# Block-wise scatters and paired turns in an expert stage, and gathers tied to the scores of the group in front

## The chip, the core and the metric

The kernel runs on one core of a Trainium2 chip. The core has five engines that work side by side, each with its own queue of instructions in a fixed order: PE (TensorE, matmuls and transposes), DVE (VectorE), ACT (ScalarE), POOL (GpSimd) and SP (SyncE, which here only issues DMAs). They wait for each other by semaphores. The metric is the time of one execution on the device, in microseconds (us); less is better.

## The reference, cut to what matters

The program is two layers of attention and feed-forward on 1024 tokens (32 sequences of 32) of 256 values, all in float32. The change lies in the last two stages. The first of these is attention over a paged cache of keys and values with a window of 128 positions, the second a mixture of 16 experts of which each token uses two, with one shared expert beside them:

```python
scores = jnp.where(allowed[:, None, None, :, :], scores, -jnp.inf)
p = jax.nn.softmax(scores, axis=-1)
o = jnp.einsum('bghts,bgsd->bghtd', p, v_all).reshape(Bx, H, Tx, HD)
...
topk_val, topk_idx = jax.lax.top_k(probs, TOPK)          # TOPK = 2, E = 16
w = topk_val / (jnp.sum(topk_val, axis=-1, keepdims=True) + EPS)
g = jnp.einsum('th,ehi->tei', xt, Wg)
u = jnp.einsum('th,ehi->tei', xt, Wu)
y = jnp.einsum('tei,eih->teh', jax.nn.silu(g) * u, Wd)
routed = jnp.einsum('tke,tk,teh->th', oh, w, y)
shared = jax.nn.silu(xt @ sWg) * (xt @ sWu) @ sWd
return (routed + shared).reshape(b, s, h)
```

## The kernel before, in words

The kernel is one unrolled program. A scheduling layer orders each engine's instructions; `behind(a, b)` (L185) tells it that b has to stand behind a on the same engine, without a semaphore, and `tc.add_manual_dep(..., waits, ...)` adds a true wait.

**The paged stage** takes 8 groups of 4 sequences. `begin(g)` issues five gathers of 128 rows of 1 KB on POOL (L1098), one for each sequence's window and one (a = 4, issued first in the code) for the new rows of all four, into a buffer `kv` of which there are four. It turns keys and queries on PE. `score` (L1157) makes the scores of one sequence, masks them on DVE, takes the exponential on ACT and lets POOL copy a part aside (`pl`, L1176). `values` turns the weights, copies them on ACT (`PT`, L1188) and multiplies by the values (L1191); `end` finishes a group (L1198 to L1225). From group 2 on, the a = 4 gather of a group waits for the first product with the values of the group two in front (`valued[g - 2]`, L1105). The gathers of groups 0 and 1 have no such wait. POOL executes its queue in order, so a gather that waits holds up every gather and `pl` copy behind it.

**The experts.** A router picks two experts for each token, which makes 2048 rows. They are sorted by expert and cut into 16 blocks of 128 rows (`NB`). A block can hold rows of several experts, so a *piece* is a block together with one expert that has rows in it; there are at most 31 (`NP` = 16 + 16 - 1), and the program always runs 31. Which block and expert a piece has is known only at run time; PE and DVE load the numbers into registers and address the weights `ew` and the rows `xT` with them. POOL picks the rows of the 16 blocks out of DRAM (`xg`, L1469, 16 indirect DMAs, nine ahead of the loop, the others in it).

The loop (from L1558, `for j in range(NP)`) does for each piece: while j < 16, two transposes of block j (`xt`, L1565) and a DVE copy to `xT` (L1567); a DVE copy of the piece's block by its register address (`xs`, L1576); two products with the gate and up weights (`gu`, L1579); silu on ACT (L1591) and the multiply on DVE (`hb`, L1592); a turn of the 128x128 result on PE (`ht`, L1594) and its copy on ACT (`hT`, L1596); the product with the down weights (`y`, L1598); a copy of that from PSUM to SBUF (`yb`, on DVE for odd j at L1601, on ACT for even j at L1603; twelve buffers). From j = 2 on POOL scatters the copy to the rows of `ys_d` in DRAM (L1608, 31 indirect DMAs). A row that is in the block but not of the piece's expert gets an index out of bounds (`SKIP`) and isn't written. `places()` works out these indices: one column for each piece.

The PSUM pool of `y` has two banks, those of `xt`, `gu` and `ht` two each; `xs` has three buffers. The order on PE in the first half is, for a pair of pieces: turn of the even piece, four transposes, product of the even piece, turn of the odd piece, product of the odd piece, eight gate and up products of the next pair.

Beside the loop runs the shared expert: `shared_in` (products `gu<-AVT,wfo`, silu, multiply) and `shared_out` (L1347, L1351) for each half of the tokens. The second half comes behind the loop. At the end 8 DMAs on the queues of SP and ACT load `ys_d` (L1628); they wait for the last scatter. DVE adds the rows by their weights (L1632), and 8 DMAs write the output (L1635).

Of the kernel before, what the change touches and what calls it, by code (L numbers as in the profile page):

```python
# [24 lines left out]
P = 128  # L25
# [103 lines left out]
def tile_layers(ctx: ExitStack, tc: tile.TileContext, i: dict, out: bass.AP):  # L129
# [916 lines left out]
    with tc.tile_pool(name="w1", bufs=1, reuse_waits="tile") as wp:  # L1046
# [31 lines left out]
        with (  # L1078
# [7 lines left out]

            valued = {}

            def begin(g):

# [4 lines left out]
                for a in (4, 0, 1, 2, 3):  # L1097
                    got = g_.indirect_dma_start(  # L1098
                        out=kv[:, a, :],
                        out_offset=None,  # L1100
                        in_=rows_d,
                        in_offset=bass.IndirectOffsetOnAxis(ap=at[:, g, a : a + 1], axis=0),
                    )
                    if a == 4 and g > 1:
                        tc.add_manual_dep(got.ins, valued[g - 2].ins.name, waits, reason="no long row of gathers")  # L1105
                q.KT = KT = sp.tile([P, 4, NPOS], F32, tag="KT", name="KT")

                def queries():
# [44 lines left out]
            def score(q, b):  # L1153

                ps = sc.tile([P, 2, NPOS], F32, tag="sc", name="sc")
                for h in range(2):
                    mm_ = te.matmul(  # L1157
                        ps[:, h, :],
                        lhsT=q.qz[:, b, h].rearrange("p g t -> p (g t)"),
                        rhs=q.KT[:, b, :],  # L1160
                        start=True,
                        stop=True,
                    )
                q.scored.append(mm_)
                sm = sp.tile([P, 2, NPOS], F32, tag="sm", name="sm", bufs=5)
                v.scalar_tensor_tensor(  # L1166
                    sm, bad[:, 4 * q.g + b, :].unsqueeze(1).broadcast_to([P, 2, NPOS]), NEG, ps, ALU.mult, ALU.add
                )
# [147 lines left out]
        with (  # L1316
# [3 lines left out]
            def small(name, shape, dt=F32):  # L1320
                return hp.tile(list(shape), dt, name=name)

            hs = small("h", (P, CH)), small("up", (P, CH))

            def shared_in(n, pool, tag, eng):
                ns = slice(n * CH, (n + 1) * CH)
                pair = []
                for f in (NE, NE + P):
                    ps = pool.tile([P, CH], F32, tag=tag, name=tag)
                    products([(ps, [(wfo[:, k, f : f + P], AVT[:, k, ns]) for k in range(2)])])  # L1330
                    pair.append(ps)
                h, up = hs if n == 0 else hs[::-1]
                silu = s.activation(h, pair[0], AF.Silu)
                for x in exps_:
                    behind(x, silu)
                if eng is g_:
                    s.copy(up, pair[1])
# [14 lines left out]

            w12 = small("w12", (P, 2, NG))
            eb = small("eb", (1, NP), I32)
            to = small("to", (P, NP), I32)
            xT = hp.tile([P, NB, D], F32, name="xT")
            with (
                tc.tile_pool(name="mm5", bufs=3, space=bass.MemoryType.PSUM, reuse_waits="tile") as mm,
# [6 lines left out]
                def rows_out(g):  # L1365

                    po = mm.tile([P, CH], F32, tag="mm", name="mm")
                    products([(po[:, :D], [(AVT[:, k, g * P : (g + 1) * P], wo2[:, k, :]) for k in range(2)])])
                    o = sp.tile([P, D], F32, tag="o", name="o")
# [143 lines left out]
            with (  # L1513
# [3 lines left out]
                tc.tile_pool(name="y5", bufs=2, space=bass.MemoryType.PSUM, reuse_waits="tile") as yp,  # L1517
            ):
                def places():

                    of = small("of", (P, NB, NE))
                    of_ = v.tensor_tensor(
                        of,
# [8 lines left out]
                    v.scalar_tensor_tensor(slot_, slot_, float(NT), tok_, ALU.mult, ALU.add)  # L1532
                    v.tensor_scalar(slot_, slot_, -SKIP, None, ALU.add)
                    mine = small("mine", (P, NP, NB))
                    v.tensor_tensor(
                        mine,
# [1 line left out]
                        C("piece").rearrange("p (j b) -> p j b", b=NB),  # L1538
                        ALU.is_equal,
                    )  # L1540
                    v.tensor_tensor(mine, mine, slot_.unsqueeze(1).broadcast_to([P, NP, NB]), ALU.mult)
                    tof = small("tof", (P, NP))
                    v.tensor_reduce(tof, mine, AX.X, ALU.add)
                    v.tensor_scalar(to, tof, SKIP, None, ALU.add)

                def weigh():

# [9 lines left out]
                put, ybs, gus = [], [], []  # L1557
                for j in range(NP):  # L1558
                    if j == 2:
                        places()  # L1560
# [33 lines left out]
                    te.transpose(ph[:, :P], h, ident)  # L1594
# [3 lines left out]
                    te.matmul(py[:, :D], lhsT=hT, rhs=w[:, 2 * D :], start=True, stop=True)  # L1598
                    yb = sp.tile([P, D], F32, tag="yb", name="yb", bufs=12)
                    if j % 2:  # L1600
                        v.tensor_copy(yb, py[:, :D])  # L1601
                    else:
                        s.copy(yb, py[:, :D])  # L1603
                    ybs.append(yb)
                    if j >= 2:
                        for k in range(len(put), j + 1):
                            put.append(
                                g_.indirect_dma_start(  # L1608
                                    out=ys_d,
                                    out_offset=bass.IndirectOffsetOnAxis(ap=to[:, k : k + 1], axis=0),  # L1610
                                    in_=ybs[k],
                                    in_offset=None,
                                    bounds_check=2 * NT - 1,
                                    oob_is_err=False,
                                )
                            )
                weigh()
                shared_out(1, shared_in(1, gp, "gu", v), yp, "y")
                behind(picked[-1], *put)
                for j, a in enumerate(put):  # L1620
                    for b in put[:j]:
                        tc.declare_no_dep(a.ins, b.ins, reason="a row is written by one piece")
# [86 lines left out]
```

## Time and profile before

| | us |
|---|---|
| runs of the kernel: median of 3 (lowest to highest) | 644.38 (643.24 to 644.47) |
| the profiled execution | 649.91 |
| its span | 647.7 |
| PE, DVE, POOL, ACT busy in the span | 579.4, 377.9, 195.7, 185.0 |
| paged stage, from its first gather to its last POOL copy | 437 to 535 |
| experts' pieces, from the first gate product to the last down product | 559 to 631 |
| loads of the scattered rows, sums and output | 634 to 647.7 |

All rows of the trace are times from the span's start in one profiled execution. A row of the timeline gives start, duration, engine, line, operation, `out<-in` by the program's names with sizes, how many, and in brackets the idle time in front of it and what ended it. PE's ends are modelled. In a float32 matmul a row often counts two passes ("x2"). A row of the windows gives what each engine was busy in a stretch, the clock that PE was granted (1.00 is full) and the share and speed of the DMA engines.

### The profile page before, as it was taken

The page shows a single profiled execution, that of the slowest core. Times are in us where ns is not written, and L with a number is a line of the kernel's source. Part 1 is how long each engine was busy: PE and PEld are TensorE (multiplying, and loading weights), DVE is VectorE, ACT ScalarE, POOL GpSimd, SP SyncE. Part 2 cuts the span into 40 slices and gives each one's busy share as a digit, 9 for nine tenths or more (in the row PEclk, how much of TensorE's full clock was granted, in tenths as well). Part 3 has the DMA queues.
Part 4 walks back from the last instruction along what each step waited for, and adds up shares of the span by engine and source line. Part 5 has one row for each costly group of instructions (what it writes and reads, how often), then busy time and mean ns, then how long its engine had stood idle before and what let it go on. Part 6 is the DMA issues. An engine that isn't in the chain of part 4 may idle for free.

```text
span 647.7 us, 9218 instructions
## 1 busy us (share of the span) xinstructions
PE 579.4 (89%) x3302; PEld 449.0 (69%) x3302; DVE 377.9 (58%) x880; ACT 185.0 (29%) x503; POOL 195.7 (30%) x279
## 2 busy tenths in 40 slices
PE   3989999999999998999999999996788889686992
PEld 1667778688778886788878886785565666464660
DVE  4656675865956939433292139554566685642535
ACT  1312232332312213122031103233456454121440
POOL 5014001523530049950000000007465300655550
PEclk9979999999999999999999999997799989797997
DMA  6962300555441000000000046014221101221115
GB/s 176 361 214 27 64 2 26 153 128 134 116 131 39 0 14 1 1 2 17 0 1 1 1 161 293 1 54 119 57 66 58 49 2 66 74 61 46 33 50 194
DMA packets 29884, 48.47 MB, mean 75 GB/s; under 512 B 8249, under 2 KB 21966, under 8 KB 29008
## 3 DMA queue, kind: packets, MB, share of 16 engines
q1 hardware_dynamic: 19405, 30.23, 13.7%
q0 software_dynamic: 5904, 15.39, 9.2%
q10 hardware_dynamic: 4531, 2.28, 1.2%
q8 instruction: 26, 0.43, 0.3%
q14 instruction: 18, 0.15, 0.1%
HBM read 36.84 MB, written 13.01 MB: 77 GB/s over the span
## 4 chain that ended last, share of the span: by engine, by line
PE 70%; DVE 16%; issue 4%; ACT 3%; DMA 3%; POOL 2%; another core or an unknown queue 1%; ACTq 0%; SPq 0%; DVEq 0%; POOLq 0%
PE ff L196 30%; PE mm L196 11%; PE gu L1579 4%; PE y L1598 3%; PE sc L1157 3%; PE tr L477 3%; DVE vblk L427 2%; PE sc L444 2%; PE po L1191 2%; PE mm L939 2%; DVE kb L437 2%; ACT sm L1172 2%; DVE AVT L1225 1%; PE tr L470 1%; POOL xg L1469 1%
## 5 line engine op out<-in xcount | busy, mean ns | idle before, releaser
L1098 POOL DMA_INDIRECT kv<-rows_d,at x40 | 39.2, 979 | 173.8 <-DVE rsm L1012 152.3
L662 POOL COPY rr<-raw 88x256 f32<-88x256 f32 x64 | 29.4, 493 | 95.8 <-PE tr L525 48.8
L594 DVE SCALAR_TENSOR_TENSOR th<-th,ff 128x512 f32<-128x512 f32 x32 | 21.8, 683 | 38.1 <-ACT th L593 38.1
L437 DVE TENSOR_TENSOR kb<-KT,con 128x1024 f32<-128x1024 f32 x28 | 34.0, 1234 | 12.3 <-ACT KT L539 6.0
L1608 POOL DMA_INDIRECT ys_d<-yb,to x31 | 30.8, 995 | 22.3 <-ACT hT L1596 7.4
L1579 PE MATMUL gu<-ew,xs 128*128 x124 | 36.4, 415 | 0.7 <-DVE xs L1576 0.7
L593 ACT ACTIVATE th<-ff 128x512 f32<-128x512 f32 x32 | 19.1, 597 | 59.5 <-PE ff L196 56.1
L196 PE MATMUL ff<-x,w_g 128*128 128x256 f32 x128 | 35.6, 391 | 0.0
L196 PE MATMUL ff<-x,w_u 128*128 128x256 f32 x128 | 34.9, 386 | 0.0
L196 PE MATMUL ff<-y,f_w_gate 128*128 128x256 f32 x128 | 31.5, 381 | 0.0
L196 PE MATMUL ff<-y,f_w_up 128*128 128x256 f32 x128 | 31.1, 381 | 0.3 <-DVE th L594 0.3
L1172 ACT ACTIVATE sm<-sm,mx 128x160 f32<-128x160 f32 x64 | 26.8, 420 | 11.7 <-DVE mx L1170 8.6
L196 PE MATMUL ff<-h,d_Wd 128*128 128x256 f32 x128 | 29.8, 381 | 0.0
L1598 PE MATMUL y<-ew,hT 128*128 x62 | 21.9, 436 | 7.7 <-issue 4.2
L196 PE MATMUL ff<-h,f_w_down 128*128 128x256 f32 x128 | 28.3, 379 | 0.0
L1157 PE MATMUL sc<-KT,qz 128*128 128x160 f32 x128 | 25.9, 335 | 2.6 <-issue 2.4
L1579 PEld LDWEIGHTS gu<-ew,xs 128*128 128x128 f32 x124 | 24.3, 209 | 5.6 <-DVE xs L1576 1.1
L1191 PE MATMUL po<-PT,kv 128*128 128x256 f32 x64 | 19.8, 432 | 9.4 <-ACT PT L1188 7.5
L1166 DVE SCALAR_TENSOR_TENSOR sm<-bad,sc 128x320 f32<-128x320 bf16 x32 | 15.5, 485 | 21.5 <-PE sc L1157 8.0
L196 PEld LDWEIGHTS ff<-x,w_g 128*128 128x128 f32 x128 | 22.8, 189 | 7.4 <-issue 4.9
L595 DVE SCALAR_TENSOR_TENSOR h<-th,ff 128x512 f32<-128x512 f32 x32 | 21.8, 680 | 9.4 <-PE ff L196 9.1
L196 PEld LDWEIGHTS ff<-x,w_u 128*128 128x128 f32 x128 | 23.5, 190 | 5.4 <-issue 2.2
(421 smaller groups left out, 1314.5 us busy)
## 6 DMA issues: line engine op xcount, KB each, us to landing
ew<-in_L_ffn_W SPq DMA_DIRECT2D x1, 6144.0 KB
rows_d<-rr SPq DMA_DIRECT2D x32, 176.0 KB
x<-in_x SPq DMA_DIRECT2D x4, 256.0 KB
w_u<-in_L_cond_Wu SPq DMA_DIRECT2D x1, 1024.0 KB
w_g<-in_L_cond_Wg SPq DMA_DIRECT2D x1, 1024.0 KB
d_Wd<-in_L_cond_Wd SPq DMA_DIRECT2D x1, 1024.0 KB
f_w_gate<-in_L_ffn_w_gate SPq DMA_DIRECT2D x1, 1024.0 KB
f_w_up<-in_L_ffn_w_up SPq DMA_DIRECT2D x1, 1024.0 KB
```

The source lines that it names most:

```text
L196: mm_ = te.matmul(ps, lhsT=a, rhs=b, start=j == 0, stop=j == len(pairs) - 1)
L437: v.tensor_tensor(kb, KT[:, m, js].rearrange("p (b k) -> p b k", b=4).unsqueeze(2).broadcast_to([P, 4, 8, 32]), m8.unsqueeze(1).unsqueeze( ...
L594: v.scalar_tensor_tensor(flat(t), flat(t), 1.0, flat(pg), ALU.add, ALU.mult)
L595: v.scalar_tensor_tensor(flat(h[:, f : f + 2]), flat(t), 0.5, flat(pu), ALU.mult, ALU.mult)
L662: g_.tensor_copy(r[:, :, j].rearrange("p o g d -> p g o d"), raw[j].rearrange("p (g a o d) -> a p g o d", g=4, a=8, d=32)[a],)
L1098: got = g_.indirect_dma_start(out=kv[:, a, :], out_offset=None, in_=rows_d, in_offset=bass.IndirectOffsetOnAxis(ap=at[:, g, a : a + 1], ax ...
L1157: mm_ = te.matmul(ps[:, h, :], lhsT=q.qz[:, b, h].rearrange("p g t -> p (g t)"), rhs=q.KT[:, b, :], start=True, stop=True,)
L1172: exp_ = s.activation(sm[:, h], sm[:, h], AF.Exp, bias=mx[:, h : h + 1], accum_out=q.su[:, b, h : h + 1])
L1191: mm_ = te.matmul(q.po[:, b, : 2 * P], lhsT=q.kv[:, b, P:], rhs=PT[:, j, :], start=True, stop=False)
L1579: mm_ = te.matmul(pg[:, :D], lhsT=x[:, 0, k * P : (k + 1) * P], rhs=w[:, k * D : (k + 1) * D], start=k == 0, stop=k == 1,)
L1598: te.matmul(py[:, :D], lhsT=hT, rhs=w[:, 2 * D :], start=True, stop=True)
L1608: g_.indirect_dma_start(out=ys_d, out_offset=bass.IndirectOffsetOnAxis(ap=to[:, k : k + 1], axis=0), in_=ybs[k], in_offset=None, bounds_ch ...
```

## The change

There are three parts.

*Scatters by block.* The result of a piece is no longer copied to a buffer of its own. A buffer `yall` of 16 blocks is set to zero by four POOL memsets ahead of the picks. Each piece's result is multiplied by a column of 0 and 1 (`own`: is the row of this piece?) and added into its block of `yall` on DVE, at an address from a register. Block b is complete with piece b + 15 at the latest, and then one scatter writes all its 128 rows; 16 scatters replace 31. `places()` gets shorter: the indices are one column for each block, without `SKIP`, and it stands one piece earlier.

*Pairs of turns.* For odd pieces up to j = 15 the turn (`ht`) has to stand ahead of the product `y` of the piece in front: turn, turn, product, product. The second half's `shared_in` products have to stand behind the last piece's product.

*Gathers.* The a = 4 gather of group 1 waits for the first score of group 0, and that of group 2 for the first score of group 1 in place of the first product with the values of group 0. The others stay.

```diff
-                    if a == 4 and g > 1:
-                        tc.add_manual_dep(got.ins, valued[g - 2].ins.name, waits, reason="no long row of gathers")
+                    if a == 4 and g:
+                        x = scored[g - 1] if g < 3 else valued[g - 2]
+                        tc.add_manual_dep(got.ins, x.ins.name, waits, reason="no long row of gathers")
...
+                scored.setdefault(q.g, mm_)
...
-                    products([(ps, [(wfo[:, k, f : f + P], AVT[:, k, ns]) for k in range(2)])])
+                    for k in range(2):
+                        up_ = te.matmul(ps, lhsT=wfo[:, k, f : f + P], rhs=AVT[:, k, ns], start=k == 0, stop=k == 1)
+                        if after:
+                            behind(after, up_)
...
-            to = small("to", (P, NP), I32)
+            to, own = small("to", (P, NB), I32), small("own", (P, NP))
+            yall = hp.tile([P, NB, D], F32, name="yall")
+            for b in range(0, NB, 4):
+                g_.memset(yall[:, b : b + 4, :], 0.0)
...
-                    v.tensor_tensor(mine, mine, slot_.unsqueeze(1).broadcast_to([P, NP, NB]), ALU.mult)
-                    tof = small("tof", (P, NP))
-                    v.tensor_reduce(tof, mine, AX.X, ALU.add)
-                    v.tensor_scalar(to, tof, SKIP, None, ALU.add)
+                    v.tensor_reduce(own, mine, AX.X, ALU.max)
+                    v.scalar_tensor_tensor(to, slot_, float(NT), tok_, ALU.mult, ALU.add)
...
-                    te.transpose(ph[:, :P], h, ident)
+                    ht_ = te.transpose(ph[:, :P], h, ident)
+                    if j % 2 and j < NB:
+                        behind(ht_, yd)
...
-                    te.matmul(py[:, :D], lhsT=hT, rhs=w[:, 2 * D :], start=True, stop=True)
-                    yb = sp.tile([P, D], F32, tag="yb", name="yb", bufs=12)
-                    if j % 2:
-                        v.tensor_copy(yb, py[:, :D])
-                    else:
-                        s.copy(yb, py[:, :D])
...
+                    yd = te.matmul(py[:, :D], lhsT=hT, rhs=w[:, 2 * D :], start=True, stop=True)
+                    ys_.append((j, at_b, py))
+                    if j == 1:
+                        places()
+                    while j >= 1 and ys_:
+                        k, at_k, py = ys_.pop(0)
+                        to_k = yall[:, bass.ds(at_k, 1), :].rearrange("p a n -> p (a n)")
+                        kept_.append(
+                            v.scalar_tensor_tensor(to_k, py[:, :D], own[:, k : k + 1], to_k, ALU.mult, ALU.add)
+                        )
+                    if j >= NE - 1:
+                        b = j - NE + 1
+                        put.append(
+                            g_.indirect_dma_start(
+                                out=ys_d,
+                                out_offset=bass.IndirectOffsetOnAxis(ap=to[:, b : b + 1], axis=0),
+                                in_=yall[:, b, :],
+                                in_offset=None,
+                            )
                         )
                 weigh()
-                shared_out(1, shared_in(1, gp, "gu", v), yp, "y")
+                shared_out(1, shared_in(1, gp, "gu", v, yd), yp, "y")
```

Two lines declare that the adds of later blocks and the scatter of an earlier one touch different rows, so that none waits for the other; the buffer `o` of the rows that are picked later now shares the three buffers of `xs`.

More of the change, by code (lines that the diff above doesn't have):

```diff
@@ L1085, in tile_layers @@
                 pass
-            valued = {}
+            scored, valued = {}, {}
             def begin(g):
@@ L1323, in tile_layers, with shared_in @@
             hs = small("h", (P, CH)), small("up", (P, CH))
-            def shared_in(n, pool, tag, eng):
+            def shared_in(n, pool, tag, eng, after=None):
                 ns = slice(n * CH, (n + 1) * CH)
@@ L1368, in rows_out @@
                     products([(po[:, :D], [(AVT[:, k, g * P : (g + 1) * P], wo2[:, k, :]) for k in range(2)])])
-                    o = sp.tile([P, D], F32, tag="o", name="o")
+                    o = sp.tile([P, 1, D], F32, tag="xs", name="o")[:, 0, :]
                     s.copy(o, po[:, :D])
@@ L1531, in places @@
                     v.tensor_tensor(pn, pn, C("block1"), ALU.add)
-                    v.scalar_tensor_tensor(slot_, slot_, float(NT), tok_, ALU.mult, ALU.add)
-                    v.tensor_scalar(slot_, slot_, -SKIP, None, ALU.add)
                     mine = small("mine", (P, NP, NB))
@@ L1555, in weigh @@
                     v.tensor_tensor(w12, w12, su.unsqueeze(1).broadcast_to([P, 2, NG]), ALU.mult)
-                put, ybs, gus = [], [], []
+                put, kept_, ys_, gus = [], [], [], []
                 for j in range(NP):
                     if j == 2:
-                        places()
                         shared_out(0, first_h, yp, "y")
@@ L1597, in tile_layers @@
                     py = yp.tile([P, CH], F32, tag="y", name="y")
-                    te.matmul(py[:, :D], lhsT=hT, rhs=w[:, 2 * D :], start=True, stop=True)
-                    yb = sp.tile([P, D], F32, tag="yb", name="yb", bufs=12)
-                    if j % 2:
-                        v.tensor_copy(yb, py[:, :D])
-                    else:
[L1603 to L1615, printed above, removed]
+                    yd = te.matmul(py[:, :D], lhsT=hT, rhs=w[:, 2 * D :], start=True, stop=True)
[16 more added lines that the diff above has]
+                                in_offset=None,
                             )
+                        )
                 weigh()
-                shared_out(1, shared_in(1, gp, "gu", v), yp, "y")
+                shared_out(1, shared_in(1, gp, "gu", v, yd), yp, "y")
                 behind(picked[-1], *put)
@@ L1621, in tile_layers @@
                     for b in put[:j]:
-                        tc.declare_no_dep(a.ins, b.ins, reason="a row is written by one piece")
+                        tc.declare_no_dep(a.ins, b.ins, reason="a row is in one block")
+                    for x in kept_[j + NE :]:
+                        tc.declare_no_dep(x.ins, a.ins, reason="a later block's rows")
                 ys = ys_d.rearrange("(k g p) d -> g p k d", k=2, p=P)
```

## The prediction

> **What bounds the kernel now.** I read the page first: PE is busy for 89% of the span and holds 70% of the chain that ended last. That is an average. The table of stretches shows the stages that the change touches (columns: PE, weight loads, DVE, ACT and POOL busy, granted clock, DMA share, GB/s):
>
> ```profile
> 437.00:470.00 33.00, 23.50 (x112) 17.54 (x111) 16.02 (x38) 13.68 (x46) 20.33 (x26) 0.79 0.31 88
> 568.60:603.00 34.40, 26.06 (x113) 18.43 (x111) 14.13 (x46) 8.10 (x30) 18.40 (x19) 0.90 0.17 54
> 603.00:628.40 25.40, 25.40 (x109) 17.33 (x109) 11.27 (x36) 11.51 (x40) 14.92 (x16) 1.00 0.13 42
> ```
>
> The rows are the start of the paged stage, the first half of the experts' pieces, and their second half. In the second half PE is never idle, at full clock. In the other two it is idle for 8 to 9 us and runs below full clock. So time can be won there, and no engine is the bound there. The timeline of the first half shows how. A pair of pieces that runs undisturbed:
>
> ```profile
> 579.01 0.32 PE L1594 MATMUL ht<-ident,hb 128*128 128x128 f32 x1
> 579.16 0.60 PE L1565 MATMUL xt<-ident,xg 128*128 128x128 f32 x4
> 579.74 0.70 PE L1598 MATMUL y<-ew,hT 128*128 x2
> 580.27 0.27 PE L1594 MATMUL ht<-ident,hb 128*128 128x128 f32 x1
> 581.06 0.70 PE L1598 MATMUL y<-ew,hT 128*128 x2 [0.52 <-ACT yb L1603]
> 581.60 1.89 PE L1579 MATMUL gu<-ew,xs 128*128 x8
> ```
>
> The next pair's first turn stands at 583.33, so a pair takes 4.32 us, 0.52 of it PE waiting for the second turned tile. Then one pair goes wrong:
>
> ```profile
> 583.77 0.99 POOL L1608 DMA_INDIRECT ys_d<-yb,to  x1 [0.30 <-issue]
> 584.06 0.70 PE L1598 MATMUL y<-ew,hT 128*128 x2
> 587.22 0.42 DVE L1567 COPY xT<-xt 128x256 f32<-128x256 f32 x1 [0.99 <-remote]
> 587.26 0.37 ACT L1603 COPY yb<-y 128x256 f32<-128x256 f32 x1 [3.26 <-remote]
> 588.34 1.22 PE L1598 MATMUL y<-ew,hT 128*128 x2 [3.48 <-issue]
> 589.36 3.62 PE L1579 MATMUL gu<-ew,xs 128*128 x8
> ```
>
> ACT's copy wants a product that PE began at 584.06 and gets it at 587.26, though ACT and DVE had nothing else to do. I call this a late handoff. PE then starves, the granted clock falls to 0.50 (587.0 to 593.5 in the windows), and eight gate products take 3.62 instead of 1.89. The next first turn stands at 594.39: the pair took 11.06 us, **6.74 more than a clean one**. What stands beside it is POOL: from 579.83 to 591.3 it issues ten scatters back to back, because the first nine had waited behind the picks (the last at 578.58). The start of the paged stage looks the same, with 14 gathers in a row:
>
> ```profile
> 453.73 0.95 POOL L1098 DMA_INDIRECT kv<-rows_d,at  x1 [0.31 <-issue]
> 457.20 0.49 DVE L1166 SCALAR_TENSOR_TENSOR sm<-bad,sc 128x320 f32<-128x320 bf16 x1 [7.58 <-remote]
> 457.26 0.59 ACT L1188 COPY PT<-tr 128x512 f32<-128x512 f32 x1 [6.01 <-remote]
> ```
>
> PE's transposes for that ACT copy ended at 453.4, so 3.8 us are lost there, and the clock after it. In 603 to 628 scatters come one per 1.65 us, each with a pause in front, and nothing is late.
>
> **Part 1, scatters by block.** 31 scatters (0.995 us each on POOL) become 16. The first stands behind piece 15, so none is issued between the last pick and about 599. The row of ten is gone. What that is worth is not in the trace; its bounds are 0, if the late handoff has another cause, and 6.74, if the row is all of it. One number pulls the value down: the profiled execution took 649.91 (span 647.7 and 2.2 around it), the runs' median is 644.38, so 5.53 us exist in the profiled execution only. The visible late time is some 17 us (8 around the gathers' row, where the first group took 21.7 us from first score to its end against 13.6 for the second; 6.7 here; about 1.2 at 570.6 to 571.8 and 1.0 at 564). If the 5.53 lies there in proportion, a third of it is not in the runs, and 6.74 becomes 4.5. **I take 4.5.**
>
> What the new bookkeeping costs: four memsets of 128x1024 on POOL. The trace has 128x128 at 0.205 and 128x1 at 0.10, so about 0.93 each, 3.7 in all, from 538.3 on (they wait for the last group's PE products). POOL is idle until its first pick at 553.42, so they are hidden by 11 us. In the placing, one 128x496 product (0.664) and two short steps go; DVE's next step there (hb at 561.26) waits for ACT anyway: nothing.
>
> 31 results are added into the block's buffer on DVE, in place of 15 DVE copies (0.424) and 16 ACT copies (0.37). The nearest row for such an add from PSUM is the shared result's at 0.421; I take 0.43. In the second half DVE has per turn 0.29 + 0.29 + 0.43 of 1.65, and the add fits between the product's end and the next copy, as yb does now at 608.82 of a turn that ends at 609.79: nothing. Each add has four register instructions ahead of it; two stand today between two xs copies that are 0.25 apart, so they cost at most 0.12 each and lie behind the step in front.
>
> **Part 2, pairs of turns.** For odd pieces up to 15 the turn (ht) stands ahead of the even piece's product. From the clean pair: ht at 579.88 (behind hb, which ends at 579.81), ACT's hT at 580.29 to 580.56, the second product at 580.61 instead of 581.06. That is 0.45 earlier. But the built order puts each add ahead of the next xs copy: the first product (580.0) ends at 580.70, its add runs 580.73 to 581.16, xs to 581.42, and the gate products start at 581.46 instead of 581.60. **0.14 a pair, seven pairs: 1.0.** The ends are 0.45 a pair (3.2) if the add is not waited for, and a loss of 0.2 a pair (1.4) if it is slower than its row. The first pair gains nothing: PE stands at 565.77 behind POOL's 1.27 us multiply as before.
>
> **Part 3, the tail.** The last shared products now stand behind the last piece's product:
>
> ```profile
> 630.25 0.59 PE L1598 MATMUL y<-ew,hT 128*128 x2
> 630.68 1.88 PE L196 MATMUL gu<-AVT,wfo 128*128 128x512 f32 x4
> 631.64 0.98 POOL L1608 DMA_INDIRECT ys_d<-yb,to  x1 [1.34 <-ACT yb L1603]
> 633.83 1.98 ACTq L1628 DMA_DIRECT2D y<-ys_d  x4
> ```
>
> The product at 630.25 had 2.05 of them around its turn; without these it starts near 629.3, and the last scatter at 630.7. Today the loads of ys_d follow that scatter by 2.19, but it moved next to nothing (0 to 2 GB/s in 631 to 634). The new one has 128 full rows. A pick of 128 rows took 2.72 from issue to its reader (554.70 to 557.42), so the loads start at 633.4: **0.4 to 0.5 won**, between 0.95 won and 0.4 lost. The shared result then ends about 0.65 later (four products of 0.86 behind 629.7), still near 636.9, when the first loaded rows are read (637.46 now).
> The Trainium skill (DMA: Bandwidth & Descriptors, Anatomy of one DMA — SWDGE (gpsimd) path) gives about 2.0 us plus bytes over 436 GB/s per DMA of this kind, which by estimate is 2.3 for 128 KB. By it the tail would win 0.8 instead of 0.5. The trace's 2.72 differs, and the sum keeps it.
>
> **Part 4, the gathers.** The dependence is given to the first gather of a group, but in the built order that gather stands last of its five (its reader's semaphore says so). For group 1 this is the tenth gather, issued at 448.71 today; the score it waits for ends at 444.9. It waits for nothing. For group 2 it is the fifteenth, 459.40 today, which would go to 462.6 behind the first score of group 1. Queued behind it on POOL are group 3's first four gathers and group 1's copies; the last gather goes from 464.98 to about 468.6 and is read at 477.7. So 13 gathers, a copy and one more stand in a row where 14 stood: **nothing**, between 3.8 won (if this shift frees the late handoff at 453.4) and 1 lost.
>
> **The sum.** 4.5 + 1.0 + 0.5 = 6.0, from 644.38: **638.4**. Against the profiled time it would be 6.74 + 1.0 + 0.5 = 8.2, so 641.7.
>
> **Rivals.** *The late handoff is not the row's* (25%). For it: two engines are released together by an event that the trace can't name, and bytes hardly moved from 582 to 586, so no queue was full. Then it stays or moves, and 1.0 + 0.5 are left: **642.9**. One such cause would be code pages that come late (44 packets on the two instruction queues); DVE gets 143 instructions more.
> The Trainium skill (Runtime: NRT & Kernel Launch, Instruction fetch mechanics) says code comes in blocks of 256 instructions and that the crossing is mostly hidden, which speaks against that cause; no run here shows a block's arrival at an engine.
> *The row moves to the busy half and is late there* (12%): 16 scatters with 128 full rows each follow PE at one per 1.65 us, where smaller ones go now. If a row of full 128 KB transfers makes handoffs late, as 14 gathers at 1.25 us apart did twice, two such losses of 4.5 come where PE has no slack: 638.4 + 9.0 = **647.4, slower**. It decides once it happens more than once. Against it: at 617 to 626 full scatters at this pace (up to 131 GB/s) made nothing late.
> *The adds bind* (8%): if add and registers take 0.85, the first xs copy comes 0.4 later and a pair costs 0.28 more than today; the second half's slack of about 0.5 is used up, say by 0.2 a turn for 15 turns. Then 644.38 - 4.5 - 0.5 + 2.0 + 3.0 = **644.4**.
>
> The forecast has 55%, its own range 634.5 to 641.7. About 0.2% (1.3 us) can be told from no change. Faster: 55%, and half of the first rival, 68%. Within: the other half and some of the last, 15%. Slower: 17%. The range for 8 in 10 runs from 635.0 to 645.5; it leaves out most of the slower rival, and the case where the gathers' late handoff goes too.
>
> **What would show it.** No 3 us hole near 584 and no clock of 0.50 from 587 to 593; pairs of 4.1 to 4.2 us; 16 scatters of about 1 us, the first near 599; turns of 1.65 in the second half; loads of ys_d about 1.8 us behind the last scatter's end; the gathers' hole at 453 to 457 still there. I am wrong if a hole of 3 us stands between 570 and 600 without a POOL row beside it, if turns grow beyond 1.65, or if the paged stage changes by over 2 us.

## The result, and the profile after

The changed kernel takes 639.2 us (median of 14 runs, 635.63 to 642.22); the kernel before took 646.04 us beside it (14 runs, 643.24 to 652.68). The ratio is **0.989, 95% interval 0.9865 to 0.9916**. The forecast was 638.4. The ratios leave out runs more than 1.5% above the fastest of their kernel, which in `row_again` (below) are five of ten. An occasion is one session in which kernels were timed beside the kernel before: on a later one the same two kernels gave 0.9994 (0.9969 to 1.0019), no change. The experiments are about that difference.

Cut at points that both profiled executions have:

| stretch | before, us | after, us |
|---|---|---|
| start to the first gather of the paged stage | 437.10 | 435.65 |
| to the first pick | 116.32 | 117.82 |
| to the third piece's turn | 15.53 | 15.67 |
| to the fifteenth piece's turn (first half) | 34.09 | 26.51 |
| to the last product `y` (second half) | 27.21 | 26.37 |
| to the end (tail) | 17.48 | 18.31 |
| span | 647.73 | 640.33 |

The table of stretches of the changed kernel (PE, weight loads, DVE, ACT, POOL busy, clock, DMA share, GB/s), for the start of the paged stage, the first half and the second half:

```profile
437.00:470.00 33.00, 22.93 (x114) 17.59 (x114) 14.77 (x36) 14.34 (x49) 19.22 (x26) 0.79 0.27 76
569.14:595.65 26.51, 24.21 (x111) 16.41 (x111) 16.72 (x51) 6.19 (x24) 4.29 (x5) 1.00 0.11 30
595.65:622.02 26.37, 25.94 (x110) 17.28 (x110) 16.11 (x45) 8.73 (x33) 13.62 (x14) 1.00 0.19 66
```

The first half has full clock now, and POOL, busy for 18.4 us in the table shown of before, is busy for 4.3. The paged stage still runs at a clock of 0.79. A pair of pieces in the timeline:

```profile
579.26 1.27 PE L1604 MATMUL y<-ew,hT 128*128 x4
...
579.93 0.48 DVE L1614 SCALAR_TENSOR_TENSOR yall<-y,own,yall 128x256 f32 x1 [0.23 <-PE y L1604]
580.34 0.28 DVE L1579 COPY xs<-xT 128x256 f32 x1
...
580.76 1.97 PE L1582 MATMUL gu<-ew,xs 128*128 x8 [0.23 <-DVE xs L1579]
...
582.57 0.32 PE L1597 MATMUL ht<-ident,hb 128*128 128x128 f32 x1
```

The two products stand side by side, and the copy `xs`, for which the gate products wait, stands behind an add. The first turns of the pairs stand at 573.86, 578.24, 582.57, 586.95, 591.27 and 595.65: 4.32 to 4.38 us a pair, where a clean pair of before took 4.32. No hole is left. In the paged stage it is still there:

```profile
452.39 0.98 POOL L1098 DMA_INDIRECT kv<-rows_d,at  x1 [0.16 <-issue]
...
455.60 0.49 DVE L1168 SCALAR_TENSOR_TENSOR sm<-bad,sc 128x320 f32<-128x320 bf16 x1 [0.37 <-remote]
455.67 0.59 ACT L1190 COPY PT<-tr 128x512 f32<-128x512 f32 x1 [6.00 <-remote]
```

And the tail:

```profile
622.02 0.70 PE L1604 MATMUL y<-ew,hT 128*128 x2 [0.41 <-issue]
...
622.56 3.60 PE L1333 MATMUL gu<-AVT,wfo 128*128 128x512 f32 x8
...
623.52 0.97 POOL L1619 DMA_INDIRECT ys_d<-yall,to  x1 [0.39 <-DVE yall L1614]
...
625.96 1.99 ACTq L1639 DMA_DIRECT2D y<-ys_d  x4
```

The shared products stand behind the last product, and the loads follow the last scatter by 2.44 (2.19 before).

**What a late handoff is.** The trace also has the times at which PE's semaphore updates arrive. This is the hole of the paged stage in the kernel before (starts of PE's matmuls that owe an update, then the arrivals, both in order):

```
451.437  PE scores L1157        457.110  update 238
452.503  PE scores L1157        457.169  update 239
452.770  PE transpose L1186     457.203  update 240
452.983  PE transpose L1186     457.237  update 241
453.197  PE transpose L1117     457.272  update 242
453.410  PE transpose L1117     457.306  update 243
453.623  PE transpose L1117     457.340  update 244
453.797  PE transpose L1117     457.374  update 245
```

PE issues the transposes 0.17 to 0.21 us apart, each of 0.42 or less. The signals come 3.3 to 5.2 us behind the ends, the last seven 0.034 us apart. So the work was issued in time, and its signals came out in one burst, closer together than PE had issued the work. That speaks for signals that were held up; as PE's ends are modelled, the trace can't rule out that the results themselves were late. "Remote" in the column of releasers is all that the page of the profile shows of it.

### The profile page after: what moved, and what is told of

It reads as the page before. It is cut to its first block, busy times and chain, and to the rows that moved or that the text cites. A ratio compares the mean times of both kernels' runs of the same rounds, so it can differ in the third digit from the quotient of the medians.

```text
span 640.3 us, 9279 instructions
## 1 busy us (share of the span) xinstructions
PE 578.5 (90%) x3302; PEld 446.6 (70%) x3302; DVE 384.1 (60%) x893; ACT 179.3 (28%) x487; POOL 184.6 (29%) x268
## 4 chain that ended last, share of the span: by engine, by line
PE 68%; DVE 17%; DMA 3%; issue 3%; ACT 3%; POOL 2%; another core or an unknown queue 1%; SPq 0%; ACTq 0%; DVEq 0%
PE ff L196 30%; PE mm L196 11%; PE gu L1582 4%; PE tr L477 3%; PE y L1604 2%; PE sc L1158 2%; DVE vblk L427 2%; DVE kb L437 2%; PE mm L939 2%; PE po L1193 2%; PE sc L444 1%; ACT sm L1174 1%; PE tr L470 1%; DVE AVT L1227 1%
## 5 line engine op out<-in xcount | busy, mean ns | idle before, releaser
L594 DVE SCALAR_TENSOR_TENSOR th<-th,ff 128x512 f32<-128x512 f32 x32 | 21.8, 682 | 38.4 <-ACT th L593 38.3
L1582 PE MATMUL gu<-ew,xs 128*128 x124 | 34.8, 401 | 2.0 <-DVE xs L1579 2.0
L1582 PEld LDWEIGHTS gu<-ew,xs 128*128 128x128 f32 x124 | 22.9, 199 | 7.7 <-PE y L1604 3.2
L196 PEld LDWEIGHTS ff<-x,w_g 128*128 128x128 f32 x128 | 22.8, 189 | 7.4 <-issue 4.9
L595 DVE SCALAR_TENSOR_TENSOR h<-th,ff 128x512 f32<-128x512 f32 x32 | 21.8, 680 | 9.4 <-PE ff L196 9.1
L196 PEld LDWEIGHTS ff<-y,f_w_up 128*128 128x128 f32 x128 | 24.0, 190 | 4.0 <-DVE th L594 0.7
L196 PEld LDWEIGHTS ff<-y,f_w_gate 128*128 128x128 f32 x128 | 24.0, 190 | 4.0 <-issue 0.8
```

Of the source, the lines that this page charges most:

```text
L196: mm_ = te.matmul(ps, lhsT=a, rhs=b, start=j == 0, stop=j == len(pairs) - 1)
L594: v.scalar_tensor_tensor(flat(t), flat(t), 1.0, flat(pg), ALU.add, ALU.mult)
L595: v.scalar_tensor_tensor(flat(h[:, f : f + 2]), flat(t), 0.5, flat(pu), ALU.mult, ALU.mult)
L1582: mm_ = te.matmul(pg[:, :D], lhsT=x[:, 0, k * P : (k + 1) * P], rhs=w[:, k * D : (k + 1) * D], start=k == 0, stop=k == 1,)
```

## The experiments

"First pick to 15th turn" is the first half with what stands ahead of it; "last group" is the first product with the values of the last of the eight groups, from the first gather on; "late" counts how often PE's updates stayed out for over 0.7 us behind a matmul that owed one. The lines are in the order of the occasions.

| kernel | ratio (95%) | last group | first pick to 15th turn | late |
|---|---|---|---|---|
| before (profile of the prediction) | | 95.9 | 49.62 | 14 |
| changed | 0.989 (0.9865 to 0.9916) | 95.1 | 42.19 | 17 |
| s_only | 0.998 (0.9953 to 1.0008) | 87.1 | 42.64 | 0 |
| t_only | 0.9971 (0.9942 to 0.9999) | 88.1 | 39.46 | 0 |
| g_only | 0.9964 (0.9934 to 0.9993) | 84.5 | 42.04 | 0 |
| no_t | 0.997 (0.9938 to 1.0002) | 84.5 | 42.63 | 0 |
| whole | 0.9994 (0.9969 to 1.0019) | 84.6 | 42.44 | 0 |
| adds_late | 0.9971 (0.9932 to 1.0009) | 84.8 | 39.82 | 0 |
| row_pool | 1.0006 (0.9974 to 1.0039) | 85.0 | 42.12 | 0 |
| g2_tied | 0.9985 (0.9954 to 1.0016) | 84.6 | 42.44 | 0 |
| row_again | 1.0049 (0.9997 to 1.0101) | 99.4 | 50.98 | 21 |
| adds_again | 0.9883 (0.983 to 0.9937) | 98.0 | 40.16 | 16 |
| both | 0.9824 (0.9783 to 0.9866) | 94.7 | 39.83 | 13 |
| row_sp | 0.9856 (0.9822 to 0.9889) | 94.8 | 42.45 | 17 |

The kernel before had a median of 646.0, 629.0, 628.7, 646.8 and 646.7 us on the five occasions (changed; s_only to no_t; whole to g2_tied; the next two; the last two). There are two kinds of occasion: those in which PE's signals come late beside POOL's DMAs, and those in which none does and the kernel before is some 17 us faster, the changed one some 12 (627.56 in place of 639.2). They belong to no one chip: the chip of `whole` to g2_tied was also that of the last two.

**The parts, one by one.** s_only is the kernel before with the scatters by block and the adds alone; no_t is the changed kernel without the line that sets the turns ahead:

```diff
-                    if j % 2 and j < NB:
-                        behind(ht_, yd)
```

> The kernel before with the scatters by block alone (adds into yall, 16 scatters, the shorter placing); turns, last shared products and gathers as before. Theory (the row of ten scatters made PE's signals late): the 3.5 us hole of PE in the first half is gone, and most of the whole gain is here: ratio 0.990 to 0.994. Rival (the late handoff has another cause and was missing in the changed kernel's profile by chance): the ratio is 0.997 to 1.003, and a hole of 2 us or more stands somewhere in 570 to 600.

> The changed kernel without the pairs of turns. If the pairs win 0.14 each as predicted, this one has pairs of 4.5 and is 1.0 us slower than the changed one (ratio to before 0.9905). If the adds eat the whole gain of the pairs, its pairs take 4.3 to 4.4 us and its ratio to before is that of the changed kernel, 0.989, within 0.001.

Neither theory of s_only stands, and neither of no_t: no hole anywhere, as the first said, but no gain of 0.6 to 1% either, because the kernel before has no hole here to lose. From the first pick to the 15th turn s_only takes 42.64, and the kernel before's own code in g_only, with 14 scatters back to back from 567.25 to 585.1, 42.04. So a row alone does not make signals late. Of the adds alone the clean pairs take 4.20 to 4.27 (s_only, no_t): 0.1 less than before, but the pair of pieces three and four takes 1.1 more (5.59 against 4.53 in g_only). The turns in pairs then add 0.1 to each clean pair and take 0.9 from that one: 42.63 without them (no_t), 42.44 with them (`whole`, below). 0.2 won in all, not 1.0. The ratio of no_t, 0.997, is that of neither of its theories, since the kernel before has no hole to lose.

t_only adds those two lines (and the names `ht_` and `yd`) to the kernel before, whose copies `yb` stay:

> The kernel before with the pairs of turns alone (the odd turn stands ahead of the even product up to j = 15). The row of ten scatters is as before. In the changed kernel a pair takes 4.33 to 4.38 us where it took 4.32 before, so the pairs' 0.45 were eaten by the adds that stand ahead of the copies xs. Here no add stands there (DVE's order is xT, xT, xs, xs, yb). Theory (the adds ate it): clean pairs of about 3.9 us, ratio 0.994 to 0.997. Rival (PE or ACT holds the pair at 4.3 anyway): clean pairs of 4.3 us, ratio 0.999 to 1.002. In both the hole beside the scatters stays.

The first theory holds for the pairs. The hole beside the scatters, which both theories expected to stay, is not there. Its timeline:

```profile
566.43 0.32 PE L1594 MATMUL ht<-ident,hb 128*128 128x128 f32 x1
...
567.45 1.27 PE L1600 MATMUL y<-ew,hT 128*128 x4
...
567.82 0.59 DVE L1576 COPY xs<-xT 128x256 f32 x2
...
568.56 1.89 PE L1579 MATMUL gu<-ew,xs 128*128 x8
...
570.29 0.32 PE L1594 MATMUL ht<-ident,hb 128*128 128x128 f32 x1
```

The copies `xs` run while PE still makes the two products, the gate products follow without a pause, and a pair takes 3.86. The pairs of turns by themselves are worth 0.46 a pair, the upper end of the prediction.

g_only has the new ties of the gathers alone:

> The kernel before with the new ties of the gathers alone. Prediction: nothing, ratio 0.998 to 1.002, and PE's hole at about 453 to 457 stays, since the tied gather is the last of its five and 13 stand in a row where 14 stood. Rival (a row shorter by one frees PE's signals): ratio 0.994 and no hole over 2 us there.

The prediction of nothing fell (no hole at 453 to 457 either), and not by the rival's reason, as the kernel before's code has no hole there on this occasion. Where signals come in time the last group is reached 2.6 to 3.6 us earlier (84.5 against 87.1 and 88.1). The old ties (in s_only) on POOL and PE:

```profile
452.17 0.95 POOL L1098 DMA_INDIRECT kv<-rows_d,at  x1 [0.30 <-issue]
453.12 0.24 POOL L1177 COPY pl<-sm 128x64 f32<-128x64 f32 x1
...
453.42 0.44 PE L1199 MATMUL tr<-ident,pl 128*128 128x128 f32 x2 [2.86 <-POOL pl L1177]
```

and the new ones (in g_only):

```profile
453.03 0.58 POOL L1178 COPY pl<-sm 128x64 f32<-128x64 f32 x3
...
453.67 0.44 PE L1200 MATMUL tr<-ident,pl 128*128 128x128 f32 x2 [0.36 <-POOL pl L1178]
```

PE waits for the copy `pl` of group 0. With the old ties it is behind 17 gathers on POOL, with the new ones behind 14: the copies are now ordered ahead of group 2's gathers, and PE waits 2.5 us less. Another 1.1 us comes from group 1: in the built order its gather of the new rows is the sixth with the old ties and the tenth with the new ones, so the four gathers of keys, for which PE waits, each come 1.25 earlier (group 0's first product with the values at 13.2 to 13.4 behind the first gather, 14.4 and 14.5 with the old ties).

**The whole change again**, unchanged, on the third occasion:

> The changed kernel itself, beside the kernel before on a second occasion. In the four runs of single parts PE's signals came in time everywhere, with rows of ten scatters and of 13 or 14 gathers as in the kernel before, and the parts were worth 0.2 to 0.4% each. Theory (the gain of 1.1% was the late handoff beside the scatters, which those runs do not have): where PE's signals come in time the whole change gives a ratio of 0.996 to 0.999, with pairs of 4.33 to 4.38 us; where they come late again, 0.987 to 0.991. Rival (the parts add up): 0.990 wherever it runs.

0.9994, just above the theory's range and with its pairs (4.32 to 4.38); the rival's 0.990 lies outside the interval. The change as a whole is worth nothing that can be measured where signals come in time. Its stages say 0.4 us lost in the first half (42.44 against 42.04) and some 3 won in the paged stage. The median is only 1.15 us lower, and the interval of the ratio is 1.6 to either side. Single runs there spread from 625 to 635 us, and the first gather alone, behind code that is not touched, came at 431.0 to 435.3 us in these eight profiles. So the stages are read, and the rest stays open.

**The row, put back.** row_pool and row_again are one kernel:

```diff
+                    if j == 7:
+                        for _ in range(10):
+                            extra = g_.indirect_dma_start(
+                                out=sp.tile([P, D], F32, tag="xg", name="extra", bufs=NB),
+                                out_offset=None,
+                                in_=od,
+                                in_offset=bass.IndirectOffsetOnAxis(ap=tok_[:, :1], axis=0),
+                            )
+                            behind(picked[-1], extra)
```

> The changed kernel with ten more picks of 128 rows in a row on POOL behind the last pick (from about 579 to 591), into buffers whose rows have been turned already: nothing reads them. Nothing else is left out or changed. It puts back a row of ten POOL DMAs in the first half. Theory (such a row makes PE's signals late, in a run in which they can be late at all): where the gathers' row of the same run shows late signals, PE has a hole of 1.5 us or more between 579 and 591 and the kernel is 2 to 7 us slower than the changed one; where the gathers show none, no hole and no loss over 0.5 us. Rival (the row plays no part): no hole in either case.

> The same kernel as row_pool (ten more picks that nothing reads, in a row on POOL behind the last pick), on another occasion, since in the first one no signal came late anywhere and no hole stood beside the row, as the theory said for such an occasion. If signals come late beside the gathers this time (group 0's first product with the values 18 us or more behind the first gather, in place of 13.3): the theory expects a hole of PE of 1.5 us or more between 579 and 591, the rival none. If they come in time: no hole again, a first half of 26.5 us, and nothing new learned about the row.

On the occasion in time the first half is that of the changed kernel, 26.63 at full clock, though POOL is busy for 13.77 of it (row_pool, and below it the kernel before's own code with its scatters, in g_only):

```profile
558.16:584.79 26.63, 24.20 (x111) 16.42 (x111) 16.59 (x51) 6.20 (x24) 13.77 (x15) 1.00 0.27 79
557.57:583.70 26.13, 23.22 (x111) 16.95 (x111) 13.83 (x45) 7.92 (x30) 17.09 (x18) 1.00 0.21 66
```

The ratio of row_pool, 1.0006 beside 0.9994, shows no loss beyond the spread. On the late occasion:

```profile
582.80 0.95 POOL L1595 DMA_INDIRECT extra<-od,tok  x1 [0.30 <-issue]
...
586.38 0.42 DVE L1570 COPY xT<-xt 128x256 f32<-128x256 f32 x1 [0.99 <-remote]
586.47 0.27 ACT L1611 COPY hT<-ht 128x128 f32<-128x128 f32 x1 [2.64 <-remote]
...
586.79 0.70 PE L1613 MATMUL y<-ew,hT 128*128 x2 [2.21 <-issue]
```

The hole is back at the same place: DVE and ACT released together by "remote", PE starved, then a granted clock of 0.82 in 579 to 592. From the first pick to the 15th turn it takes 50.98, against 42.19 without the row: 8.8 us, more than the scatters' row cost (7.4), with DMAs that nothing waits for. adds_again, on the same occasion and without such a row, takes 40.16. The theory holds in kind: where signals can be late, a row of POOL DMAs beside the pieces makes them late. The cost is above its 2 to 7 us: 8.8 here, and 1.6% (some 10 us) between the ratios 1.0049 and 0.989, which stem from two occasions.

row_sp asks whether any traffic does it. The ten loads have the same size and the same buffers, but come from SP's queue:

```diff
+                            extra = nc.sync.dma_start(sp.tile([P, D], F32, tag="xg", name="extra", bufs=NB), od[:P, :])
+                            tc.add_manual_dep(extra.ins, mm_.ins.name, waits, reason="where the row stands")
```

> The changed kernel with ten more loads of 128 rows from SP's queue at the place where row_pool has its ten picks: the same bytes into the same buffers, nothing reads them, but POOL issues none. Where signals come late beside the gathers: if POOL's issuing (or its kind of DMA) makes them late, the first half stays at 26.5 us; if any DMA traffic beside PE does, it grows by 2 us or more, as with row_pool (35.0). Where they come in time: 26.5 us, and the question stays open.

The profile is one of late signals (17, and 20.6 us to group 0's first product with the values). SP issues the row, and the stretch from the third turn to the 15th:

```profile
573.36 4.91 SPq L1595 DMA_DIRECT2D extra<-od  x10
```

```profile
564.07:590.57 26.50, 24.23 (x111) 16.39 (x111) 16.49 (x51) 6.21 (x24) 4.30 (x5) 1.00 0.25 79
```

No hole, at up to 462 GB/s from 575 on. The row is shorter in time than POOL's (the loads are issued in 5 us, not 12.5), so this clears the traffic, not every kind of DMA from SP; and whether it is POOL's issuing or its indirect kind of DMA that counts was not tried.

**The adds behind the copies.** adds_late and adds_again are one kernel, the changed one with

```diff
-                    v.tensor_copy(x, xT[:, bass.ds(at_b, 1), :])
+                    cp_ = v.tensor_copy(x, xT[:, bass.ds(at_b, 1), :])
+                    if 2 <= j < NB:
+                        behind(cp_, *kept_[j // 2 * 2 - 2 : j // 2 * 2])
```

> The changed kernel with the adds of a pair put behind the next pair's copies xs on DVE. Without adds, pairs of turns gave pairs of 3.86 us; with adds in front of xs, 4.33 to 4.38. Theory (the adds in front of xs hold the gate products): pairs of 3.9 to 4.0 us, 2.5 to 3.2 us faster than the changed kernel. Rival (DVE's time for the adds binds, wherever they stand): pairs of 4.2 or more, under 1 us faster.

> The same kernel as adds_late, measured again because the spread of single times (4 us on either side, most of it ahead of the stages that are changed) hid a gain of 3 us. From the stages: 2.6 us less than the changed kernel from the first pick to the end, and some 3 us less than before in the paged stage: ratio 0.990 to 0.996. If DVE's adds cost something that the stages don't show: 0.997 to 1.000.

The pair, in adds_again:

```profile
578.71 0.49 DVE L1579 COPY xs<-xT 128x256 f32 x2
...
579.46 1.89 PE L1584 MATMUL gu<-ew,xs 128*128 x8
579.49 1.07 DVE L1616 SCALAR_TENSOR_TENSOR yall<-y,own,yall 128x256 f32 x2 [0.29 <-issue]
```

The adds run beside the gate products, the pair takes 3.86, and from the first pick to the 15th turn 2.6 us are won in time (42.44 to 39.82) and 2.0 late (42.19 to 40.16). The medians don't show it apart from their spread (0.9971 beside 0.9994, 0.9883 beside 0.989): the theory is shown by the stages, not by the ratios. The range that was expected of adds_again, 0.990 to 0.996, was missed too: its 0.9883 is that of a late occasion.

**The gathers' row.** g2_tied ties all five gathers of group 2; `both` adds the edit of adds_late to it:

```diff
-                    if a == 4 and g:
-                        x = scored[g - 1] if g < 3 else valued[g - 2]
+                    if (a == 4 or g == 2) and g:
+                        x = scored[g - 1] if g == 1 else valued[g - 2]
```

> The changed kernel with all five gathers of group 2 tied to the first product with the values of group 0, so that ten stand in a row and then a pause, in place of 13, a copy and one more. Theory where PE's signals come late: the hole of 3.6 us at 452 to 456 shrinks below 1.5 and the kernel is 2 to 4 us faster than the changed one; where they come in time: no gain, since nothing is late there, and up to 1 us lost if group 2's keys come late. Rival: the hole stays the same.

> The two edits that the runs point to, together: the adds behind the copies xs (2.6 us less in the pieces), and group 2's five gathers tied to the first product with the values of group 0 (ten gathers in a row, then a pause). Where signals come in time: ratio 0.990 to 0.997, the paged stage as in the changed kernel. Theory where they come late: the hole beside gathers 10 to 14 (PE's signals 3.8 to 5.2 us late) becomes under 2 us and the ratio is 0.980 to 0.986. Rival (ten in a row are enough to make them as late): the hole stays, ratio 0.987 to 0.990.

In time it wins nothing: a wait of PE of 2.65 for `pl` now stands in group 1. On the late occasion `both` is faster than the kernel before (0.9824) and, by its median, than row_sp, the changed kernel with ten loads more (635.17 against 636.53 us, 0.9824 against 0.9856: the intervals overlap), but in the paged stage the hole only moved:

```profile
448.33 1.13 PE L1193 MATMUL po<-PT,kv 128*128 128x256 f32 x4 [0.15 <-ACT PT L1190]
...
462.85 0.47 PE L1112 MATMUL tr<-ident,qall 128*128 128x128 f32 x1 [5.06 <-ACT PT L1190]
```

Group 0's product waits 0.15 us where it waited 3.6, at 15.4 behind the first gather in place of 20.7. Then POOL issues the next eight gathers from 450.70 on with one copy between, and PE waits 5.06 for the next group. The last group is reached at 94.7, as in the changed kernel (95.1). My expectation of a hole under 2 us holds for the row that was cut, and not for the stage. The ratio lies in the theory's range, but by the stages the gain is that of the adds alone (39.83 against 42.45 in row_sp, with the last group at 94.7 and 94.8).

## Why the prediction was right, point by point

- **The late handoff of the scatters' row, 4.5.** Right in place and cause, too small. The first half fell from 34.09 to 26.51. The clean first half of the old code is 26.13 (g_only), so the holes cost 7.96 there: the 6.74 of the pair shown, and 1.2 at 570.6 to 571.8. That second hole stands beside picks, which the changed kernel has as well, so that it is gone is not shown to be the change's doing. For the 6.74 the step that failed is the scaling. "5.53 us exist in the profiled execution only" was read from three runs; 14 runs lie between 643.24 and 652.68, and the profiled 649.91 lies among them.
- **The row as its cause.** Not shown by the profile of before, and a rival had 25%. row_again shows it, with the condition that the profile could not show: the occasion. (The row was read a little long: nine scatters stand back to back from 579.83 to 591.3, right behind the pick at 578.58, and the tenth follows at 592.30 behind a pause of 1.0.) In the six late profiles together PE's updates stayed out for over 0.7 us 98 times, and each of the 98 has a POOL DMA issued between 4 us before the update was due and its arrival, while of all updates of these profiles only about half have one so near. Between 240 and 435 us of the kernel before, where POOL issues none, all 108 updates came in time.
- **Late code.** In row_sp three packets of the instruction queues come between 575 and 590 us, and no signal is late there; in row_again, with its hole, there is one. The Trainium skill (Runtime: NRT & Kernel Launch, Instruction fetch mechanics) says that crossing a block is mostly hidden; the stretch of row_sp agrees.
- **Pairs of turns, 1.0.** Wrong: the clean pairs won nothing (4.36 on the mean of five, in place of 4.32), and the pair of pieces three and four, of which it expected the same 0.14, was 0.9 shorter for it (4.72 in `whole`, 5.59 in no_t). The order on DVE was read rightly (add ahead of `xs`), and the rest came as worked out up to the gate products, which start 2.52 behind the pair's first turn (2.45 predicted). Then eight of them take 1.97 behind a pause of 0.23, where they took 1.89 without one in before. The 0.14 was smaller than what the sum left out. The upper bound of 0.45 was the true worth of the edit without the adds (0.46 in t_only).
- **The tail, 0.4 to 0.5.** From the fifteenth turn to the end it took 44.70 before and 44.68 after. 0.84 is won ahead of the last product as said; 0.10 goes to the add in front of the last scatter, 0.26 to the scatter of full rows (2.44 from its issue to the loads; a pick gave 2.72), and 0.47 behind the loads. That last one is the step that failed: the shared result was to end 0.65 later and still ahead of the first loaded rows. Counted from the fifteenth turn its adds end 1.86 later (33.18 before, 35.04 after), the last two behind the first loaded row (629.54), and when the second half of the loads has come DVE has nine of its sixteen additions left, not eight. On occasions in time the same stretch took 45.04 in g_only and 44.52 in `whole`: 0.5.
- **The gathers, nothing.** Late: the last group 0.8 us earlier, and a clock of 0.50 at 532 to 539 took it back before the first pick (117.82 against 116.32). The way from the last group to the first pick goes with that clock in all profiles: 19.9 to 20.4 us where full clock was granted all along, 21.2 to 21.8 with one step of 3.41 us at 0.50 in it, 22.6 to 22.8 with two. In time: 2.6 to 3.6 won, more than the 2 us by which the prediction itself would call this part wrong. What failed is the list of what is queued behind the tied gather. It looked for a later hole and a later last gather, not for the copies of group 0 that come ahead. And it took group 1's gather of the new rows for the tenth in the kernel before; the semaphore that its reader waits for there is the sixth gather's, and the new tie is what moves it to the tenth place.
- **Placing, memsets, second half, nothing each.** Right. The memsets took 3.62 from 538.10, the first pick stands at 553.47, and the turns are 1.65 with scatters of 0.96 to 1.01. One reading of the first table is a little off: PE is idle for 9.5 us in the paged stretch (33.00 less 23.50), not 8 to 9.
- **The row in the busy half (12%).** PE's updates are late there too (up to 1.2 us, at 601 and 621), but the time shows nothing of it: 26.37 late, 26.34 in time. That the pauses between scatters, a turn's slack of some 0.5 and the two banks cover it is likely, and not tried.

That the sum of 6.0 came near the 6.84 between the medians (7.40 between the two spans) is in part luck: a term too small by 3.5 was offset by 1.4 of pairs and 0.5 of tail that were not there, and the change was timed on an occasion of the kind that the profile of before shows. Of the 7.40, 1.45 lie ahead of the first gather, in code that is not touched, and 1.50 are lost again between it and the first pick.

## What to carry to other kernels

When two engines are released together with nothing to name as releaser, look at when the producer's semaphore updates arrive, and at what GpSimd issues beside it: here ten of its DMAs in a row cost 8 us on an occasion with late signals, and the same bytes from another queue nothing. Before a term is put on such a hole, see whether it is there on another occasion, for the change is worth 1.1% on one kind and nothing that can be measured on the other. And on an in-order engine, put what is not needed yet behind what the bound engine waits for: the adds behind `xs` won 0.5 us a pair (4.36 to 3.86), a later group's gathers behind `pl` 2.5 us in the paged stage.

## What the runs showed of the hardware that was not expected

- PE's semaphore updates arrived up to 5.2 us behind their matmuls' modelled ends beside POOL's indirect DMAs, and then 0.034 us apart. On two occasions of five none of some 575 updates a profile was late, with the same rows. What differs between the occasions is open. The late profiles also miss 7 to 9% of PE's updates (539 of 579 recorded in before), the others none; whether that is the same cause was not tried.
- The Trainium skill (SBUF — State Buffer, SBUF: two separate sides) says "A DMA cannot be slowed by a compute op, and vice versa". It excepts GpSimd's DMAs, as the side that a DVE operation holds up. The page speaks of the ports of the memory, and no run here shows whether these are what is held. What is measured goes the other way round: GpSimd's DMAs hold up what follows PE's matmuls, and the clean pair of 4.32 us became 11.06. The page's remedy for its own case, another queue, fits this one too (row_sp: 26.50).
- A granted clock of 0.50 stands beside or right behind each long hole, for 3.4 to 13.7 us in steps of 3.41, which is part of why a wait of 3.48 us cost 6.74.
